# Batch 0's attention in a fused attention-and-convolution kernel: denominators, inverses and bias moved to other places in the order

## The chip, the cores and the metric

The kernel runs on one core of one Trainium2 chip. The metric is the device time of one execution in microseconds (us). The engines of the core work side by side, each through its own queue in order: TensorE (PE, matmuls), VectorE (DVE), ScalarE (ACT), GpSimd (POOL), and SyncE (SP), which issues transfers. ScalarE's and GpSimd's queues issue transfers as well. Engines wait for each other by semaphores.

## The reference

Two layers on an input of 4 images, 1024 channels, 32 x 32 pixels, all in float32. Cut to what matters:

```
# layer 0: self-attention over the 1024 pixels of each image, 16 heads of 64
qkv = x @ w_qkv.T + b_qkv
q, k = rmsnorm(rope(q)) * q_norm_w, rmsnorm(rope(k)) * k_norm_w
scores = einsum("bqhd,bkhd->bhqk", q, k) * hd**-0.5
ctx = einsum("bhqk,bkhd->bqhd", softmax(scores), v)
x = rmsnorm(ctx @ w_proj.T) * norm_out_w + x
# layer 1: bottleneck of convolutions 1x1, 3x3, 1x1
y = relu(bn(conv1x1(x, w1))); y = relu(bn(conv3x3(y, w2)))
x = relu(x + softplus(residual_scale) * bn(conv1x1(y, w3)))
```

The change touches the softmax and what follows it. The kernel computes exp(scores) without a shift, sums the exponentials over the keys (the denominator), multiplies the context by the inverse of the denominator, and adds the bias of v last, since the weights of a softmax sum to one.

## The kernel before

**Stages.** For each batch b of four, the kernel projects to q, k and v, runs the attention, and projects the context (y). Projections are done with fewer multiplications, by sums of operand and weight blocks formed on VectorE beforehand. Layer 1 follows after the four batches.

**Attention.** `attention` is called for each half c of the 1024 queries (`half[c]`, 512 queries), and loops over eight pairs of heads `hp`. One pass over (c, hp) is called a unit here; a batch has 16, numbered 0 to 15. In a unit, for eight tiles t of 128 keys, TensorE writes scores `sc` (L781), ScalarE exponentiates them to `p` (L788), and VectorE adds the tiles up to `den` (L799, L801). Then TensorE forms the contexts `cx` from v and p (L810). Two halves of the keys give two partial contexts: ScalarE copies the first to q's place (L816), and the second is copied and added by a GpSimd transfer (L819, L820), or, in the last unit, added by VectorE out of the context bank (L845).

**Denominators.** After every odd unit the sums of two units are a group. `sums_of_four` multiplies them with ones on TensorE (`dn`, L863). For most groups `inverses` does this: the step is put into `late`, and is run at tile t = 1 of the next unit. ScalarE copies the result (`rec`, L910), SP sends four rows to memory and reads them back spread over the partitions (`to_few`), VectorE inverts the few numbers (L914), and SP writes them back and broadcasts them to `inv` (`spread`, L932). The inversion waits in `half_done` until the end of a unit. `ready` then holds the broadcast rows, and at the end of the next odd unit `mean_of_v` multiplies the context by them on VectorE (L764) and adds v's bias on GpSimd (L765). The last group of the batch (`last_inverses`) inverts in place on VectorE (L924), and its means are formed in the projection (`means`, on VectorE).

**The projection's order.** `project2` issues products of eight matmuls each, counts half a unit of pace for each (`product_done`), and runs steps when their pace has come (`after`). In the first products: `start(0)` (bank p1, first ring of banks o1), `second(0)` (p2, ring o2), then the loop's first product into p1 and p5 (o2).

**Buffers.** PSUM has eight banks. In the attention three score tiles of two banks and a context tile of two use them all (`psum_for("att")`). The projections use two rings of four (`o1`, `o2`) in the same banks. The sums of a unit have two buffers in the pool `acc` ("tot"), and the exponentials have one buffer for each tile t, so that the next unit overwrites them.

**Other work in the stretch.** Batch 0's attention also prepares weights for later projections: `load_parts` (t = 3) loads four pieces over SP, and at a unit's end `extra` forms four sums on VectorE (L392 to L395), which GpSimd sends to memory (L397).

**What sets the order.** TensorE, GpSimd, VectorE and ScalarE run in the order in which the program is written there. SP's order is set by a scheduler when the program is built.

Of the kernel before, what the change touches and what calls it, by code (L numbers as in the profile page):

```python
# [11 lines left out]
F32 = mybir.dt.float32  # L12
AF = mybir.ActivationFunctionType
ALU = mybir.AluOpType
# [4 lines left out]
P = 128  # L19
# [4 lines left out]
NHP = C // (2 * HD)  # L24
CH = 512
NCH = N // CH
# [35 lines left out]
NH = NT // 2  # L62
# [23 lines left out]
def program(ctx, tc, x, wblk, w2, w3, vecs, cos, sin, out, bad):  # L86


    nc = tc.nc
# [26 lines left out]
    def col(name, i=0):  # L116
        return vec[:, COL[name] + i : COL[name] + i + 1]
# [40 lines left out]
    with tc.tile_pool(name=f"st{u}", bufs=2) as st, ExitStack() as s:  # L158

        tp = s.enter_context(tc.tile_pool(name=f"tp{u}", bufs=1))  # L160
# [24 lines left out]
        half = [slice(c * CH, (c + 1) * CH) for c in range(NCH)]  # L185
# [17 lines left out]
        def bank(kind, name):  # L203
            pool, shape = psum[kind]
            return pool.tile(shape, F32, tag=kind, name=name)
# [48 lines left out]
        def after(n, step):  # L254
            later.append((pace["at"] + n, step))
# [505 lines left out]
        def mean_of_v(q_all, c, hp, w, engine=nc.gpsimd):  # L761

            cx = q_all[:, hp, half[c]]
            nc.vector.tensor_tensor(cx, cx, w, ALU.mult)  # L764
            engine.tensor_scalar(cx, cx, col("bv", hp), None, ALU.add)  # L765

        def attention(b, c, q_all, k_all, v, probs_, late, ready, extra, slow, steps_in_all, load_parts, fold, then):


            at = half[c]  # L770
            sums_, contexts = [], []
            for hp in range(NHP):
                n = f"{b}_{c}_{hp}"
                rows = shifts(q_all, k_all, n, hp, c) if bad is None else None
                probs = []
                for t in range(N // P):
                    p = probs_[:, t]
                    sc = bank("sc", f"sc_{n}_{t}")
                    for keys in (low, high):
                        for j, d in enumerate((low, high)):  # L780
                            nc.tensor.matmul(  # L781
                                sc[keys, j], k_all[d, hp, t * P + keys.start : t * P + keys.stop], q_all[d, hp, at],
                                start=True, stop=bad is not None,
                            )
                    if bad is None:
                        for j in range(2):
                            nc.tensor.matmul(sc[:, j], ones[0:1, :], rows[j], start=False, stop=True)
                    nc.scalar.activation(p, sc, AF.Exp)  # L788
                    if t == 1:
                        if late:  # L790
                            late.pop(0)()
                        if fold and hp % 2 == 0:
                            d_ = fold[hp // 4][:, hp % 4 // 2 * 2 : hp % 4 // 2 * 2 + 2, :]
                        else:
                            d_ = acc.tile([P, 2, CH], F32, tag="tot", name=f"den_{n}")
                    if t == 3:
                        load_parts()
                    if t == 1:
                        nc.vector.tensor_tensor(d_, probs[0], p, ALU.add)  # L799
                    elif t > 1:  # L800
                        nc.vector.tensor_tensor(d_, d_, p, ALU.add)  # L801
                    probs.append(p)
                if (c, hp) == (NCH - 1, NHP - 1):
                    then()
                o = bank("cx", f"cx_{n}")
                for t in range(N // P):
                    for j in range(2):
                        h0 = (2 * hp + j) * HD
                        for i, keys in enumerate((low, high)):
                            nc.tensor.matmul(  # L810
                                o[j * HD : (j + 1) * HD, i], v[keys, t, h0 : h0 + HD], probs[t][keys, j],
                                start=(t == 0), stop=(t == N // P - 1),
                            )

                cx = q_all[:, hp, at]
                nc.scalar.copy(cx, o[:, 0])  # L816
                if b == 0 and (c, hp) != (NCH - 1, NHP - 1):
                    other = temp(f"cx_{n}")
                    nc.scalar.copy(other, o[:, 1])  # L819
                    nc.gpsimd.dma_start(cx, other, accum_op=ALU.add)  # L820
                else:
                    contexts.append((cx, o[:, 1]))
                sums_.append(d_)
                if hp % 2 == 1:
                    for r in ready:
                        mean_of_v(q_all, *r)
                    ready.clear()
                if fold:
                    halve(hp, d_, fold[hp // 4][:, hp % 4 // 2 * 2 : hp % 4 // 2 * 2 + 2, :])
                    if hp % 4 == 3:  # L830
                        eights.append((hp + 2, lambda n=n, hp=hp: sum_of_eight(b, n, hp, fold[hp // 4], ready)))
                if half_done and half_done[0][0] <= c * NHP + hp:
                    half_done.pop(0)[1]()
                if slow:
                    slow.pop(0)()

                if waiting:
                    next_waiting()
                slots = NCH * NHP - 1
                if extra and steps_in_all == 0 and hp > 0:  # L840
                    extra.pop(0)()
                for _ in range(len(extra) - -(-steps_in_all * max(slots - 1 - c * NHP - hp, 0) // slots) if steps_in_all else 0):
                    extra.pop(0)()
                if contexts:
                    nc.vector.tensor_tensor(contexts[0][0], *contexts.pop(0), ALU.add)  # L845
                if eights and eights[0][0] <= c * NHP + hp:
                    eights.pop(0)[1]()
                if hp % 2 == 0 or fold:
                    continue
                if (c, hp) == (NCH - 1, NHP - 1):  # L850
                    last_inverses(b, c, hp, n, sums_of_four(n, sums_), ready)
                else:
                    late.append(lambda n=n, hp=hp, ds=sums_: inverses(b, c, hp, n, sums_of_four(n, ds), ready))
                sums_ = []

        def sums_of_four(n, sums_):
            if n == f"0_{NCH - 1}_{NHP - 1}":
                bank("sc", f"skip_{n}")
            dn = bank("sc", f"dn_{n}")[:, 0]
            for i, d_ in enumerate(sums_):  # L860
                for j in range(2):
                    q = slice((2 * i + j) * QH, (2 * i + j + 1) * QH)
                    nc.tensor.matmul(dn[q, :], ones[:, :QH], d_[:, j], start=True, stop=True)  # L863
            return dn

        half_done, eights = [], []
        low, high = slice(0, P // 2), slice(P // 2, P)

        def halve(hp, d_, home):
# [35 lines left out]
        def inverses(b, c, hp, n, dn, ready):  # L905


            r = temp(f"rec_{n}")
            k = 2 * ((b * NCH + c) * NHP + hp - 1)
            nc.scalar.copy(r, dn)  # L910
            few, rows = to_few(n, k, 4, r[::QH, :])

            def invert():
                nc.vector.reciprocal(few, few)  # L914
                nc.sync.dma_start(rows, few)
                spread(c, hp, n, ready, [dens[k + j : k + j + 3 : 2, :] for j in range(2)])

            half_done.append((0, invert))

        def last_inverses(b, c, hp, n, dn, ready):  # L920
            k = 2 * ((b * NCH + c) * NHP + hp - 1)
            r = temp(f"rec_{n}")
            nc.scalar.copy(r, dn)
            nc.vector.reciprocal(r, r)  # L924
            nc.gpsimd.dma_start(dens[k : k + 4, :], r[::QH, :])
            spread(c, hp, n, ready, [dens[k + j : k + j + 3 : 2, :] for j in range(2)], nc.gpsimd)
# [271 lines left out]
        for b in range(B):  # L1198
# [29 lines left out]
            v = room  # L1228
# [30 lines left out]
            slow = [lambda: None] * 3 + [lambda f=f: add_residual(f) for f in range(NT)] if b > 0 else []  # L1259
            probs_ = xp.tile([P, N // P, 2, CH], F32, tag="x", name=f"p_{b}")  # L1260
            fold = [None, None]
            if b > 0:

                fold[0] = [tp.tile([P, NH, CH], F32, tag=t, name=f"den_{b}_{t}") for t in ("T0", "T2")]
# [8 lines left out]
            for c in range(NCH):  # L1273
                if (b, c) == (B - 1, NCH - 1):
                    extra = filters()
                attention(
                    b, c, q_all, k_all, v, probs_, late, ready, extra, slow, steps_in_all, load_parts, fold[c], then
                )
            psum_for("proj")
            room = v_room(f"to_{b}")  # L1280
# [50 lines left out]
        w = conv1_weights("last")  # L1331
# [364 lines left out]
```

## Time and profile before

| | us |
|---|---|
| median of three runs | 2651.2 |
| lowest and highest | 2650.92, 2652.52 |
| the profiled execution | 2650.94 |
| its span, first to last instruction | 2649.1 |
| batch 0's first score matmul (in the span) | 285.44 |
| batch 0's last context matmul group, start | 507.08 |
| first matmul of batch 0's output projection | 517.37 |

Times in the timelines count from the span's start. A line of a timeline gives the start, the duration from the first to the last end of the merged instructions, the engine, the line of the program, the operation with output and inputs, and in brackets the idle time before it and what ended that. Matmuls overlap: the next one starts before the one ahead has ended, so that the distance from start to start says more than a duration. In the page, a group's line ends with its idle time and the engine that ended most of it.

The table of waits of VectorE between 285 and 520 us (who waited for what: total us, times, longest):

```profile
DVE few L914 <- DMA few<-densf: 2.2, 2, 1.7
DVE w_pre L392 <- DMA w_pre<-in_wblk_dram: 2.2, 2, 1.2
```

VectorE waited four times in the whole stretch, for transfers alone.

### The profile page before, as it was taken

The numbers are of one execution on the slowest core, as the hardware profiler recorded it, in microseconds if no ns is written. First come the engines' busy times: TensorE is split into PE (matmuls) and PEld (weight loads), VectorE is DVE, ScalarE is ACT, GpSimd is POOL, SyncE is SP. The second block draws the span as 40 slices with busy tenths as digits, with TensorE's granted clock in tenths as the row PEclk, the third lists the DMA queues.
The fourth block names the chain that finished last, engine by engine and source line by source line (L and its number), as shares of the span: only waits on it lengthen the run. The fifth ranks groups of instructions, "written<-read, shape, count | busy, mean of one in ns | idle before, by whom it ended". The sixth has DMA issues, their size and how long they took to land. (4 is left out here: it accounts for less than half of the span.)

```text
span 2649.1 us, 40551 instructions
## 1 busy us (share of the span) xinstructions
PE 2626.4 (99%) x15446; PEld 1627.8 (61%) x15446; DVE 2143.2 (81%) x2595; ACT 1120.7 (42%) x1568; POOL 472.1 (18%) x592
## 2 busy tenths in 40 slices
PE   9999999999999999999999999999999999999997
PEld 4448533488888333688886333888884335846843
DVE  5567899998887877888879767987988779877987
ACT  2222566423442565333343565233525564312266
POOL 2542244301011221100111222000111221020000
PEclk9999999999999999999999999999999999999999
DMA  8887787777667451457775541765774443683175
GB/s 286 289 255 204 218 257 239 245 221 238 185 181 212 87 102 41 143 173 225 190 200 143 93 86 26 223 206 174 193 214 86 82 104 90 208 279 92 64 240 205
DMA packets 252939, 463.66 MB, mean 175 GB/s; under 512 B 32193, under 2 KB 125169, under 8 KB 252737
## 3 DMA queue, kind: packets, MB, share of 16 engines
q1 hardware_dynamic: 196816, 287.80, 34.7%
q0 software_dynamic: 47856, 156.40, 23.7%
q10 hardware_dynamic: 8064, 16.78, 1.8%
q8 instruction: 125, 2.05, 0.3%
q14 instruction: 78, 0.63, 0.1%
HBM read 329.53 MB, written 97.01 MB: 161 GB/s over the span
## 5 line engine op out<-in xcount | busy, mean ns | idle before, releaser
L788 ACT ACTIVATE p<-sc 128x1024 f32<-128x1024 f32 x512 | 478.2, 1047 | 17.7 <-PE sc L781 17.5
L781 PE MATMUL sc<-q,k 64*64 64x512 f32 x4096 | 456.4, 591 | 0.0
L801 DVE TENSOR_TENSOR den<-den,p 128x1024 f32<-128x1024 f32 x312 | 385.5, 1236 | 37.6 <-ACT p L788 5.1
L810 PE MATMUL cx<-p,to 64*64 64x512 f32 x3072 | 338.2, 589 | 0.0
L781 PEld LDWEIGHTS sc<-q,k 64*64 64x64 f32 x4096 | 149.3, 132 | 294.2 <-ACT p L788 150.6
L810 PEld LDWEIGHTS cx<-p,to 64*64 64x64 f32 x3072 | 117.5, 133 | 212.1 <-issue 210.8
L480 PE MATMUL p_v<-w_v,x 128*128 128x256 f32 x928 | 210.2, 379 | 1.4 <-DVE x L451 0.7
L485 PE MATMUL p_y<-q,w_y 128*128 128x256 f32 x928 | 209.8, 379 | 0.7 <-issue 0.7
L485 PEld LDWEIGHTS p_y<-q,w_y 128*128 128x128 f32 x928 | 176.0, 190 | 27.9 <-issue 4.1
L480 PEld LDWEIGHTS p_v<-w_v,x 128*128 128x128 f32 x928 | 176.1, 190 | 26.8 <-DVE x L451 1.7
L816 ACT COPY q<-cx 128x512 f32<-128x512 f32 x64 | 37.5, 586 | 348.0 <-PE cx L810 348.0
L765 POOL TENSOR_SCALAR q<-q,vec 128x512 f32<-128x512 f32 x56 | 110.1, 1985 | 290.2 <-DVE q L764 290.2
L485 PE MATMUL p_q<-to,w_q 128*128 128x256 f32 x672 | 152.2, 379 | 0.0
L485 PE MATMUL p_k<-to,w_k 128*128 128x256 f32 x672 | 152.2, 379 | 0.0
L485 PEld LDWEIGHTS p_q<-to,w_q 128*128 128x128 f32 x672 | 127.4, 190 | 18.4 <-issue 1.2
L485 PEld LDWEIGHTS p_k<-to,w_k 128*128 128x128 f32 x672 | 127.4, 190 | 18.4 <-issue 1.2
L810 PE MATMUL cx<-p,rq 64*64 64x512 f32 x1024 | 112.7, 589 | 0.0
L1600 PE MATMUL c<-h,w 128*128 128x512 f32 x256 | 110.3, 592 | 0.5 <-ACT h L1503 0.5
L799 DVE TENSOR_TENSOR den<-p 128x1024 f32<-128x1024 f32 x52 | 63.5, 1222 | 42.6 <-ACT p L788 42.6
L801 DVE TENSOR_TENSOR den_T<-den_T,p 128x1024 f32<-128x1024 f32 x72 | 88.2, 1225 | 7.5
L485 PE MATMUL p_y<-to,w_y 128*128 128x256 f32 x384 | 90.1, 379 | 0.6 <-PE p_y L485 0.6
L727 POOL DMA_DIRECT2D k<-ks x64 | 57.9, 1093 | 181.6 <-ACT p L788 70.9
(499 smaller groups left out, 4340.0 us busy)
## 6 DMA issues: line engine op xcount, KB each, us to landing
w_v<-wd2f SPq DMA_DIRECT2D x112, 256.0 KB, 3.2
w_y<-wd2f SPq DMA_DIRECT2D x112, 256.0 KB, 3.3
w_q<-wd2f SPq DMA_DIRECT2D x84, 256.0 KB, 3.0
w_k<-wd2f SPq DMA_DIRECT2D x84, 256.0 KB, 2.9
wd2f<-w_pre POOLq DMA_DIRECT2D x68, 256.0 KB, 4.5
q<-qs POOLq DMA_DIRECT2D x64, 256.0 KB, 5.5
k<-ks POOLq DMA_DIRECT2D x64, 256.0 KB, 4.7
x1df<-y POOLq DMA_DIRECT2D x32, 512.0 KB, 5.2
```

The costliest lines, as they stand in the source:

```text
L480: nc.tensor.matmul(o[:, q].rearrange("p (g f) -> p g f", g=2), r[:, i, q * P : (q + 1) * P], wt[:, :, i, :], skip_group_check=True, **at,)
L485: nc.tensor.matmul(o[:, q], wt[:, q, i, :], r[:, i, :], skip_group_check=True, **at)
L727: nc.gpsimd.dma_start(dst[i::2, f, :], other[1 - i :: 2, :], accum_op=ALU.add)
L765: engine.tensor_scalar(cx, cx, col("bv", hp), None, ALU.add)
L781: nc.tensor.matmul(sc[keys, j], k_all[d, hp, t * P + keys.start : t * P + keys.stop], q_all[d, hp, at], start=True, stop=bad is not None,)
L788: nc.scalar.activation(p, sc, AF.Exp)
L799: nc.vector.tensor_tensor(d_, probs[0], p, ALU.add)
L801: nc.vector.tensor_tensor(d_, d_, p, ALU.add)
L810: nc.tensor.matmul(o[j * HD : (j + 1) * HD, i], v[keys, t, h0 : h0 + HD], probs[t][keys, j], start=(t == 0), stop=(t == N // P - 1),)
L816: nc.scalar.copy(cx, o[:, 0])
L1600: nc.tensor.matmul(os[i], w3t[k][f // NH][:, f % NH, :], h2[b, k][:, half[c]], start=(k == 0), stop=(k == NPT - 1),)
```

## The change

All of it is in batch 0's attention and in the start of its projection; the other batches keep their order.

- The groups' denominators are formed after score tile t = 3 of the next unit in place of t = 1, but for the group whose next unit is 14.
- The sums of batch 0 get four buffers of their own, `own`, in the room of T0 and T2 (which hold operand sums of the projections before and after).
- The inversion of the few numbers comes at tile t = 2 of the odd unit after next, in place of the end of the unit before that; for the group of unit 13 it stays at the end of unit 14.
- The context is multiplied by the inverses at the end of even units in place of odd ones. The bias of v is added by ScalarE, behind the exponentials of tiles 5 and 6 of the next unit (`biases`). The group that is used in the last unit gets both steps from VectorE there.
- The last group's sums, inverses and broadcast (`last`) are put half a unit of pace into the projection, that is after its first product. Its sums go to a bank of the ring o2 in place of one of the score banks.

```diff
-        def attention(..., fold, then):
+        def attention(..., fold, then, own):
 ...
                     nc.scalar.activation(p, sc, AF.Exp)
+                    if t == (3 if b == 0 and (c, hp) != (NCH - 1, NHP - 2) else 1) and late:
+                        late.pop(0)()
+                    if t in (5, 6) and biases:
+                        biases.pop(0)()
+                    if b == 0 and t == 2 and half_done and half_done[0][0] < c * NHP + hp:
+                        half_done.pop(0)[1]()
                     if t == 1:
-                        if late:
-                            late.pop(0)()
-                        if fold and hp % 2 == 0:
+                        if b == 0:
+                            d_ = own[hp % 4 // 2][:, hp % 2 * 2 : hp % 2 * 2 + 2, :]
+                        elif fold and hp % 2 == 0:
 ...
-                if hp % 2 == 1:
+                if hp % 2 == min(b, 1) or (c, hp) == (NCH - 1, NHP - 1):
                     for r in ready:
-                        mean_of_v(q_all, *r)
+                        if b > 0:
+                            mean_of_v(q_all, *r)
+                        elif (c, hp) == (NCH - 1, NHP - 1):
+                            mean_of_v(q_all, *r, nc.vector)
+                        else:
+                            mean_and_bias(q_all, *r)
                     ready.clear()
 ...
                 if (c, hp) == (NCH - 1, NHP - 1):
-                    last_inverses(b, c, hp, n, sums_of_four(n, sums_), ready)
+
+                    def last(ds=sums_):
+                        last_inverses(b, c, hp, n, sums_of_four(n, ds), ready)
+
+                    if b == 0:
+                        after(0.5, last)
+                    else:
+                        last()
 ...
         def sums_of_four(n, sums_):
             if n == f"0_{NCH - 1}_{NHP - 1}":
-                bank("sc", f"skip_{n}")
-            dn = bank("sc", f"dn_{n}")[:, 0]
+                dn = bank("o2", f"dn_{n}")
+            else:
+                dn = bank("sc", f"dn_{n}")[:, 0]
 ...
-        half_done, eights = [], []
+        half_done, eights, biases = [], [], []
+
+        def mean_and_bias(q_all, c, hp, w):
+            cx = q_all[:, hp, half[c]]
+            nc.vector.tensor_tensor(cx, cx, w, ALU.mult)
+            biases.append(lambda: nc.scalar.activation(cx, cx, AF.Identity, bias=col("bv", hp)))
+
 ...
-            half_done.append((0, invert))
+            half_done.append((c * NHP + hp + (1.5 if hp < NHP - 3 or c < NCH - 1 else 1) if b == 0 else 0, invert))
 ...
+            own = None
+            if b == 0:
+                own = [tp.tile([P, NH, CH], F32, tag=t, name=f"den_{b}_{t}") for t in ("T0", "T2")]
```

More of the change, by code (lines that the diff above doesn't have):

```diff
@@ L765, in mean_of_v, with attention @@
             engine.tensor_scalar(cx, cx, col("bv", hp), None, ALU.add)
-        def attention(b, c, q_all, k_all, v, probs_, late, ready, extra, slow, steps_in_all, load_parts, fold, then):
+        def attention(b, c, q_all, k_all, v, probs_, late, ready, extra, slow, steps_in_all, load_parts, fold, then, own):
             at = half[c]
@@ L1276, in program @@
                 attention(
-                    b, c, q_all, k_all, v, probs_, late, ready, extra, slow, steps_in_all, load_parts, fold[c], then
+                    b, c, q_all, k_all, v, probs_, late, ready, extra, slow, steps_in_all, load_parts, fold[c], then, own
                 )
```

## The prediction

> **What bounds the kernel now.** I read the page first (busy shares, chain), then TensorE's waits, then the timelines of the five engines over batch 0's attention and the start of its projection, because the diff changes nothing else. The page:
>
> ```profile
> span 2649.1 us, 40551 instructions
> PE 2626.4 (99%) x15446; PEld 1627.8 (61%) x15446; DVE 2143.2 (81%) x2595; ACT 1120.7 (42%) x1568; POOL 472.1 (18%) x592
> ```
>
> TensorE is idle for 2649.1 - 2626.4 = 22.7 us in all, so a change that removes no TensorE work can gain only out of such gaps. Where they lie in the changed stretch, TensorE's timeline says (start, duration, instruction, idle before and its releaser):
>
> ```profile
> 343.54 1.07 PE L863 MATMUL dn<-den,ones 128*32 128x512 f32 x8
> 372.17 1.50 PE L863 MATMUL dn<-den,ones 128*32 128x512 f32 x8
> 373.60 5.38 PE L781 MATMUL sc<-q,k 64*64 64x512 f32 x48
> ...
> 507.08 7.05 PE L810 MATMUL cx<-p,rq 64*64 64x512 f32 x64
> 514.06 1.05 PE L863 MATMUL dn<-den,ones 128*32 128x512 f32 x4
> 515.58 1.05 PE L863 MATMUL dn<-den,ones 128*32 128x512 f32 x4 [0.47 <-DVE den L801]
> 517.37 3.69 PE L485 MATMUL p_y<-q,w_y 128*128 128x256 f32 x16 [0.73 <-issue]
> ```
>
> I number the 16 passes over (c, hp) as units 0 to 15. A denominator group normally takes 1.06 us with its pipelined tail and 1.0 us from start to start; only the one at 372.17 holds a wait of 0.43 us. The last group ought to end at 514.06 + 1.0 = 515.06 and the projection start then; it starts at 517.37. So 2.31 us are lost at the seam: 1.02 waiting for unit 15's denominators on VectorE, 1.29 until ScalarE's copy of the sums. Together 2.74 us is **all** there is to win here. The seam on VectorE and ScalarE:
>
> ```profile
> 507.65 7.87 DVE L801 TENSOR_TENSOR den<-den,p 128x1024 f32<-128x1024 f32 x6
> 515.44 0.69 DVE L450 TENSOR_TENSOR y<-q 128x512 f32<-128x512 f32 x1
> ...
> 518.05 1.29 DVE L764 TENSOR_TENSOR q<-q,inv 128x512 f32<-128x512 f32 x2
> 519.25 0.68 DVE L845 TENSOR_TENSOR q<-q,cx 128x512 f32<-128x512 f32 x1
> 519.85 3.35 DVE L924 RECIPROCAL rec<-rec 128x512 f32<-128x512 f32 x1
> ```
>
> ```profile
> 516.68 0.59 ACT L923 COPY rec<-dn 128x512 f32<-128x512 f32 x1 [1.90 <-PE dn L863]
> ```
>
> VectorE runs without a gap from 417.5 to 531; L845, which empties the last context bank, ends at 519.93. That number decides below.
>
> **What the Trainium skill says.** "SBUF — State Buffer", section "SBUF: two separate sides": VectorE and GpSimd share a port pair, an exclusive lock for the whole instruction when the VectorE operation has two SBUF inputs and the GpSimd one reads SBUF. The trace agrees: a 128x512 weight addition takes 0.69 us, but beside GpSimd's L765 it takes 1.05 to 1.18:
>
> ```profile
> 487.91 1.18 DVE L392 TENSOR_TENSOR w_pre<-w_pre,w_pre 128x512 f32<-128x512 f32 x1
> 489.12 0.69 DVE L393 TENSOR_TENSOR w_pre<-w_pre,w_pre 128x512 f32<-128x512 f32 x1
> 489.85 1.06 DVE L394 TENSOR_TENSOR w_pre<-w_pre,w_pre 128x512 f32<-128x512 f32 x1
> ```
>
> "ScalarE: Activation LUTs", section "Table sets: the hidden batching unit": cheap functions such as identity are in every set, so a bias between exponentials loads no table. No Identity stands between exponentials in this trace; the changed program's order shows no load added there. "Perfetto Trace Analysis", section "Identifying the Most-Contended Engine": matmul busy time is a poor measure, as matmuls are pipelined. The trace agrees: the seam's two idle marks say 1.20 us where start-to-start times say 2.31.
>
> **The change, part by part.** *Denominators at score tile 3 instead of 1* (six groups; the seventh, in unit 14, stays at tile 1). TensorE does the same matmuls. At 372.17 unit 5's sums were ready at 364.69 + 7.87 = 372.56; two tiles later the group starts at about 373.9, so 0.43 us goes and nothing takes its place. The other five cost and gain nothing. Cover: the group takes one of three score banks and its copy (0.6 us) stands behind two more exponentials. Exponentials follow each other by 7.46/8 = 0.93 us, score tiles by 6.87/8 = 0.86; the first starts 486.52 - 485.31 = 1.2 us after its unit. Counting from there, the exponential of tile 3 ends near 5.0, the copy near 5.5, and tile 6, which takes the copied bank, wants it at 6.15. If that 0.6 us of cover went, at most 0.2 to 0.3 us per group would show, 6 times.
>
> *Own buffers for the sums* (T0, T2) cost nothing: four instead of two, free since the value projection, and read out by 517, while the next batch writes them at 550.
>
> *Few inverses and their use later.* Per group the same small reciprocal (0.25 us), pair of multiplications (1.2 us) and five SP transfers (rows out, few in, few out, two broadcasts). The reciprocal now stands after tile 1's addition of the next odd unit, so VectorE's two waits for few (2.2 us) go. On SP the few transfers move past weight loads. The nearest case: the part that VectorE wants at 487.91 is loaded from 478.68 on, 8 transfers in 6.80 us with about 3 us to landing (as the page has it for w_y), so its four are there by about 485. VectorE will be there near 484.6, and needn't be before 485.3. Cover about 1 us; if gone, VectorE idles 1 to 2 us. The broadcast rows are wanted 15 us after their reciprocal and take about 9.
>
> *Bias of v by ScalarE.* 14 GpSimd operations of 1.97 us become 12 ScalarE ones and 2 VectorE ones. The nearest ScalarE row with a vector operand is L611 sq_q<-q,vec, 0.72 us; from below, the copies of L816, 0.59. I take 0.65, as neighbours overlap a little. They stand behind exponentials 5 and 6 of odd units, 1.3 us per unit, where ScalarE then sits idle for 5.3 us before the next context. The last tile is exponentiated near 10.1 us after the unit's start and wanted by the contexts at 6.87 + 7 x 0.86 = 12.9. Cost: nothing. Gain: VectorE's collisions. After its last wait (417.5) they cost 1.05 + 1.06 + 1.05 + 1.06 + 1.18 + 1.06 - 6 x 0.69 = 2.3 us before unit 15's sums are done, so these end at 515.52 - 2.3 = 513.2. From the other side: unit 14's sums can't start before its second exponential, about 3.25 us after the unit's start; its start (485.31 - 0.43) + 3.25 + 9.1 (sums) + 1.4 (multiplications, few) + 5.5 (two weight parts) + 9.1 = 513.2 too. Bounds: 512.1 (unit 15's own second exponential) and 515.5 (no gain).
>
> *Last group in the projection.* TensorE leaves the contexts at 514.06 - 0.43 = 513.63. The projection's first product needs no ScalarE copy now, and runs 1.73 us to 515.36; then the denominators, whose inputs are ready, to 516.36. They take the first bank of the second ring, so the **second product** gets the bank after it, which lies over the last context bank: in the changed program it waits for L845. Before the change that bank went to p5 (L563 on), three products further on at 517.37 + 3 x 1.73 = 522.6, when L845 was long done. L845 is itself later in VectorE's queue: the two bias operations of group 13 now stand ahead of it. Four such operations take 534.38 - 532.13 = 2.25 us in the later means, where two multiplications took 1.20, so 1.05 more. From the end of the sums to the end of L845 it was 519.93 - 515.52 = 4.41, and becomes 5.46. L845 ends at 513.2 + 5.46 = 518.66, and the second product starts near 518.75. Before, it started at 517.37 + 1.73 = 519.10. Queued behind this wait is the whole projection. **Net: 0.35 us gained**; 2.4 us of new waiting eats most of the 2.74.
>
> After that nothing is late: VectorE's long reciprocal starts near 518.7 (before 519.85), so the chain to the last means (VectorE waited 1.1 us at 532.13) is about 1 us earlier, TensorE only 0.35.
>
> Sum: the profiled execution took 2650.94 us (span 2649.1 and 1.84 around it), 0.26 below the median of 2651.2. 2651.2 - 0.35 = 2650.85, say 2650.9.
>
> **Rivals.** *The gate stays, and VectorE is not earlier* (slower). If removing GpSimd's reads frees nothing, or a weight part or the few of unit 14 (issued behind four weight loads on SP) come late by as much, unit 15's sums end at 515.5, L845 at 520.98, and the second product starts 1.95 us later than before: 2653.1. It decides from the point where L845 ends after 519.0. For it: the gap-free VectorE and the 1.05 us added to its queue. Against it: the collisions are in the trace, and the unit-14 account has its own bound.
>
> *No gate* (faster): if the second product didn't wait for L845, it would start at 516.36, 2.74 us earlier: 2648.5. For it: every removed wait is real. Against it: the wait stands in the changed program, and VectorE can't end L845 before 512.1 + 5.46 = 517.6, which leaves 1.45 us at best (2649.7).
>
> *The biases hold up the exponentials*: if they hit at every odd unit from 5 to 15 with the 1.3 us uncovered, 6 x 1.3 = 7.8 us: 2658.6. Only 2.8 us of cover speaks against it, but that is twice the cost.
>
> **How the numbers follow.** Gate with an earlier VectorE 0.62 (2649.6 to 2652.0); gate with VectorE as before 0.21; no gate 0.11; exponentials held up, or another wait above 5 us, 0.06. The range 2649.3 to 2653.4 takes in the first two and leaves out most of the rest. A difference of 0.2% is 5.3 us, about what a measurement of this kernel can tell from no change. All 2.74 us together are 0.10%, so faster by more needs a gap that this profile doesn't show: 0.02. Slower by more needs L845 after 524.4 or uncovered biases: 0.05. Within: 0.93.
>
> **What would show it.** Right: every denominator group at 1.06 us; no GpSimd L765 in batch 0 and weight additions at 0.69; one TensorE wait of 2 to 3 us for VectorE's L845 (L856 in the new numbering) in front of the second product, near 518.7. Wrong: that product near 516.4 (no gate) or near 521 (no earlier VectorE); TensorE gaps in score tiles of odd units; VectorE waiting for weight parts.

## The result, and the profile after

The changed kernel takes 2656.64 us (median of 22 runs, 2653.0 to 2660.61), the kernel before 2652.68 us beside it (22 runs, 2650.88 to 2655.74). The ratio is 1.0015, with a 95% interval of 1.0010 to 1.0021: about 4 us slower. That lies inside the 0.2% which the prediction calls about what can be told from no change, but outside its range of 2649.3 to 2653.4. The profiled execution of the changed kernel took 2655.39 us, 1.8 of it around this span:

```profile
span 2653.6 us, 40533 instructions
PE 2629.0 (99%) x15446; PEld 1629.8 (61%) x15446; DVE 2140.1 (81%) x2597; ACT 1127.5 (42%) x1580; POOL 446.9 (17%) x578
```

The span is 4.5 us longer. TensorE's busy time has grown by 2.6 us although it does the same 15446 matmuls. So a part of the loss is not waiting: the matmuls themselves took longer. TensorE's table of waits over the whole span (who waited for what: total us, times, longest) has one new entry of weight, and it is the first:

```profile
PE p_y L485 <- DVE q L856: 4.3, 1, 4.3
PE c2x L1489 <- DVE V L1424: 1.5, 2, 1.0
...
PE p_y L485 <- DMA w_y<-in_wblk_dram: 0.4, 1, 0.4
```

TensorE's timeline at the seam between attention and projection:

```profile
506.17 7.05 PE L816 MATMUL cx<-p,rq 64*64 64x512 f32 x64
513.63 1.97 PE L485 MATMUL p_y<-q,w_y 128*128 128x256 f32 x8 [0.42 <-DMA w_y<-in_wblk_dram]
515.53 1.81 PE L882 MATMUL dn<-den_T,ones 128*32 128x512 f32 x8
521.65 3.78 PE L485 MATMUL p_y<-q,w_y 128*128 128x256 f32 x8 [4.32 <-DVE q L856]
525.23 4.90 PE L485 MATMUL p_y<-y,w_y 128*128 128x256 f32 x16
529.96 1.89 PE L485 MATMUL p_y<-q,w_y 128*128 128x256 f32 x8
```

The first product, the denominators and then the second product behind the gate L856 stand where the prediction put them. But the second product starts at 521.65 in place of 518.75. And it takes 525.23 - 521.65 = 3.58 us from start to start, where a product takes 1.73; the next two take 529.96 - 525.23 = 4.73 in place of 3.45. The table by stretches says why. Each line gives a stretch and its length, then each engine's busy time in it, and in the column PEclk the granted TensorE clock. The stretches are cut where the record of the clock can step, every 3.41 us in this trace (the last section shows it); such a stretch is called a window from here on:

```profile
core 0: us, PE busy (x) PEld busy (x) DVE busy (x) ACT busy (x) POOL busy (x), PEclk, DMA share, GB/s
517.57:520.98 3.41, 0.00 (x0) 0.00 (x0) 3.34 (x7) 0.40 (x1) 0.00 (x0) 1.00 0.47 162
520.98:524.40 3.42, 2.75 (x7) 2.21 (x8) 3.42 (x3) 0.00 (x0) 0.00 (x0) 0.50 0.02 5
524.40:527.81 3.41, 3.41 (x10) 2.69 (x9) 3.38 (x4) 0.00 (x0) 0.58 (x1) 0.50 0.34 79
527.81:531.22 3.41, 3.41 (x17) 3.02 (x16) 3.28 (x5) 1.17 (x2) 1.21 (x2) 1.00 0.52 142
```

Behind a window without TensorE work the clock is at half for two windows, 6.83 us. The kernel before, with its two short waits at the seam, keeps it:

```profile
513.00:517.37 4.37, 3.17 (x21) 0.48 (x13) 4.16 (x5) 1.17 (x2) 0.00 (x0) 1.00 0.99 347
517.37:522.60 5.23, 5.23 (x24) 4.63 (x25) 5.23 (x6) 0.59 (x1) 3.48 (x2) 1.00 0.46 133
```

VectorE, whose L856 is the gate, shows no collision any more, but waits for transfers:

```profile
485.91 0.69 DVE L392 TENSOR_TENSOR w_pre<-w_pre,w_pre 128x512 f32<-128x512 f32 x1 [1.86 <-DMA w_pre<-wdf]
...
501.36 0.25 DVE L939 RECIPROCAL few<-few 128x16 f32<-128x16 f32 x1 [2.26 <-DMA few<-densf]
...
508.36 7.87 DVE L807 TENSOR_TENSOR den_T<-den_T,p 128x1024 f32<-128x1024 f32 x6
...
520.92 0.68 DVE L856 TENSOR_TENSOR q<-q,cx 128x512 f32<-128x512 f32 x1
```

The sums of unit 15 end at 508.36 + 7.87 = 516.2, and L856 at 521.6. The wait of 2.26 us is followed up on SP's queue, first after the change, then before it:

```profile
485.92 7.74 SPq L383 DMA_DIRECT2D w_pre<-wdf  x4
493.76 0.54 SPq L923 DMA_DIRECT2D densf<-rec  x1
494.42 1.63 SPq L383 DMA_DIRECT2D w_pre<-wdf  x3
496.37 0.33 SPq L927 DMA_DIRECT2D few<-densf  x1
```

```profile
488.98 0.53 SPq L898 DMA_DIRECT2D densf<-rec  x1
493.62 2.00 SPq L383 DMA_DIRECT2D w_pre<-wdf  x3
495.71 0.48 SPq L902 DMA_DIRECT2D few<-densf  x1
```

ScalarE had the sums (rec) of the group of unit 13 ready at 488.0. But they were issued at 493.76 only, since they stood on SP behind a weight load that waited for its buffer. Before the change they went out at 488.98. Even so the few themselves were read back only 0.66 us later than before (496.37 against 495.71), as then too they had stood behind weight loads. The larger part of the wait is that VectorE now came for them earlier: at 499.10, where before it came at 500.66 and found them there.

**One reading aid for what follows.** In a few of the profiled executions the stretch ahead of the attention runs up to 2 us longer: the changed kernel's first score matmul stands at 284.97 in one execution and at 287.05 in another, before the change at 285.44. So places at the seam are given here as distances from the first score matmul of batch 0. The n-th matmul of one trace is set against the n-th of another, with the denominators left out, as they were moved. "Fifth product" is the one at 524.35 in the kernel before.

| us after the first score matmul | first product | second | fifth | second to fifth |
|---|---|---|---|---|
| before | 231.93 | 233.73 | 238.91 | 5.18 |
| after | 228.67 | 236.69 | 244.99 | 8.30 |
| after, profiled again | 228.33 | 235.96 | 243.62 | 7.66 |

The gate costs 2.2 to 3.0 us at the second product; from the second to the fifth another 2.5 to 3.1 are lost to the clock. This agrees with the record of the clock: TensorE worked 2.75 + 3.41 = 6.16 us at half clock in the first trace and 1.44 + 3.42 = 4.86 us in the second (shown below), and half of that is 3.1 and 2.4. In the changed kernel's first trace the fifth product, by absolute times, is 5.6 us late and the last matmul 4.5. Most of that 1.1 is no gain of the change: the output projection of batch 3 lost it in the profiled execution of before (the matched difference falls from 5.62 to 4.55 between 2221 and 2246 us there), and the other traces, of kernels with and without the change, lack most of that loss too.

### The profile page after: what moved, and what is told of

It is laid out like the page before. It is cut to its first block, busy times and chain, and to the rows that moved or that the text cites. A ratio compares the mean times of both kernels' runs of the same rounds, so it can differ in the third digit from the quotient of the medians.

```text
span 2653.6 us, 40533 instructions
## 1 busy us (share of the span) xinstructions
PE 2629.0 (99%) x15446; PEld 1629.8 (61%) x15446; DVE 2140.1 (81%) x2597; ACT 1127.5 (42%) x1580; POOL 446.9 (17%) x578
## 5 line engine op out<-in xcount | busy, mean ns | idle before, releaser
L807 DVE TENSOR_TENSOR den<-den,p 128x1024 f32<-128x1024 f32 x216 | 267.6, 1239 | 27.6 <-ACT p L788 5.6
L807 DVE TENSOR_TENSOR den_T<-den_T,p 128x1024 f32<-128x1024 f32 x168 | 205.8, 1225 | 17.2 <-DVE den_T L807 0.5
L765 POOL TENSOR_SCALAR q<-q,vec 128x512 f32<-128x512 f32 x42 | 83.6, 2000 | 278.6 <-DVE q L764 278.6
L480 PE MATMUL p_v<-w_v,t 128*128 128x256 f32 x384 | 90.1, 379 | 0.0
```

What stands on the lines that cost most here:

```text
L480: nc.tensor.matmul(o[:, q].rearrange("p (g f) -> p g f", g=2), r[:, i, q * P : (q + 1) * P], wt[:, :, i, :], skip_group_check=True, **at,)
```

## The experiments

Theory 1 is the reading above: the loss is the gate, and the half clock that follows the idle stretch it makes. The rivals: the dip of the clock has nothing to do with the idle; the loss lies in the steps moved inside the attention, or in VectorE's new waits. All times are medians beside runs of the kernel before on the same chip. "Low clock" counts the runs whose mean clock over the span is 0.997 or less; 6.83 us at half clock take 3.4 of 2650 us, 0.0013, off the mean, and 3.41 us take 0.0006. In all 14 traces the mark is right (0.9963 to 0.9975 in the five with such a dip inside the span, 0.9975 to 0.9981 in the nine without), but for a short dip only narrowly. Before the change 3 of 169 runs are low.

| | edit on | us against before | ratio, 95% | second to fifth | low clock |
|---|---|---|---|---|---|
| after | - | +3.96 | 1.0015 (1.0010 to 1.0021) | 8.30 | 20 of 22 |
| after again | - | +3.45 | 1.0014 (1.0007 to 1.0021) | 7.66 | 18 of 19 |
| 32 fillers | after | +2.92 | 1.0014 (1.0007 to 1.0020) | 5.28 | 2 of 21 |
| 14 fillers | after | +0.47 | 1.0003 (0.9994 to 1.0011) | 5.29 | 2 of 13 |
| gate off | after | +1.70 | 1.0006 (1.0000 to 1.0013) | 5.28 | 5 of 21 |
| last group back | after | -0.20 | 1.0001 (0.9992 to 1.0009) | 5.18 | 1 of 13 |
| only last group | before | +0.69 | 1.0002 (0.9994 to 1.0011) | 5.26 | 4 of 13 |
| context first | after | -0.25 | 0.9999 (0.9990 to 1.0007) | 5.28 | 2 of 13 |
| few by GpSimd | after | +5.08 | 1.0019 (1.0011 to 1.0027) | 5.28 | 12 of 13 |
| all of these | after | +2.99 | 1.0013 (1.0006 to 1.0019) | - | 6 of 21 |
| no gate, SP kept | after | +1.21 | 1.0007 (1.0000 to 1.0013) | - | 6 of 21 |
| few by GpSimd | before | +1.63 | 1.0012 (1.0005 to 1.0019) | 5.18 | 10 of 21 |
| seam mended | before | -1.15 | 0.9998 (0.9990 to 1.0006) | - | 1 of 13 |

(In the three rows with "-" the denominators stand between these products.)

### The changed kernel again

> The changed kernel itself, beside the others on one chip. All theories: +3.5 to +4.5 us against the kernel before, mean clock 0.997 or less in most runs.

+3.45 us, 18 of 19 runs low. Its trace repeats the gate to the hundredth (4.32 us), and the half clock with it:

```profile
517.63:521.04 3.41, 1.06 (x8) 0.14 (x4) 3.34 (x6) 0.95 (x2) 0.00 (x0) 1.00 0.81 262
521.04:524.45 3.41, 1.44 (x4) 1.17 (x4) 3.38 (x5) 0.00 (x0) 0.00 (x0) 0.50 0.02 5
524.45:527.87 3.42, 3.42 (x10) 2.67 (x9) 3.38 (x3) 0.00 (x0) 0.58 (x1) 0.50 0.02 7
```

The loss is no accident of one execution. Here TensorE had still worked 1.06 us in the window ahead of the dip.

### Keep TensorE busy during the wait

```diff
                 dn = bank("o2", f"dn_{n}")
+                for _ in range(32):
+                    nc.tensor.matmul(dn[:, :P], ones, ones, start=True, stop=True)
```

> The changed kernel with 32 small matmuls of ones (128x128) put ahead of the last group's denominators, in the bank that these overwrite; the outputs are the same. They keep TensorE busy for about 3.4 us of the 4.3 us in which it waited for VectorE's L856. Theory 1 (the loss is the later second product, +2.55 us, plus a halved clock that follows an idle of over about 4 us, 3.1 us): the second product still starts near 521.6, the longest idle before it falls below 2 us, the granted clock stays at 1.0 behind it, and the time falls by about 3 us against the change, to the kernel before +0.5 to +1.5 us. Theory 2 (the dip of the clock has nothing to do with the idle, or the loss comes from the moved steps inside the attention): no gain, +4 us as in the change. Theory 3 (only the gate counts, the clock is made good later): also +4 us, but with the clock at 1.0.

The 32 matmuls took 7.31 us, twice the intended (the trace shows each as two records), and outlasted the gate: the second product started at 238.31. No dip followed (5.28 from second to fifth), but the fillers themselves gave the saving back: +2.92. Inconclusive for the time; for the clock it speaks for theory 1. Hence the same with 14:

> As the first filling run, with 14 small matmuls in place of 32 (32 took 7.31 us and overran the gate by some 3 us; 14 should take 3.2 us, and end before L856). Theory 1 (late second product plus halved clock after the idle): second product at the same distance from the start of the attention as in the change (236.7 us after the first score matmul, against 233.7 in the kernel before), idle before it about 2 us, mean clock 0.998 in nearly all runs where the change has 0.997 or less in 20 of 22, time about 3 us under the change: +0.5 to +1.5 us against the kernel before. Theory 2 (the clock does not matter, the later product does all): +3 to +4 us.

```profile
513.86 1.97 PE L485 MATMUL p_y<-q,w_y 128*128 128x256 f32 x8
515.66 3.29 PE L878 MATMUL dn<-ones 128*128 128x128 f32 x28
518.88 1.06 PE L884 MATMUL dn<-den_T,ones 128*32 128x512 f32 x8
520.62 1.99 PE L485 MATMUL p_y<-q,w_y 128*128 128x256 f32 x8 [0.67 <-DVE q L856]
```

The gate is still there, and the second product still late: 235.15, 1.4 us behind the kernel before. (It came 0.8 and 1.5 us earlier than in the two traces of the changed kernel, as VectorE waited only 0.65 us for few in this execution.) But TensorE computed through the wait, and the next products go at full speed: 5.29 us from second to fifth in place of 8.30 and 7.66, and 2 of 13 runs low in place of 20 of 22. The time is back to +0.47. These matmuls do nothing for the result, and the time falls by about 3 us: **the idle brings the dip**. The intervals of the two ratios still touch (0.9994 to 1.0011 against 1.0007 to 1.0021), so the clock counts and the traces carry this more than the time does. What a dip costs shows also with the program unchanged: in the five kernels of the table with at least four low runs and at least nine others, the low runs' median is 1.5 to 4.6 us above that of the others (a longer wait ahead of the dip may have a share in that).

### Take the gate away, or open it earlier

Another ring for the last denominators, so that the second product no longer gets the bank of the last context:

```diff
-                dn = bank("o2", f"dn_{n}")
+                dn = bank("o1", f"dn_{n}")
```

> The changed kernel with the last group's denominators in a bank of the first ring (o1) in place of the second (o2), so that the second product no longer lies over the last context bank; that bank then goes to p5, two products further on. Theory 1: the second product starts near 517.4 (behind the denominators, which wait for VectorE's sums until 516.2), p5 near 521.7 behind a wait of about 0.8 us, the clock stays at 1.0, and the time is about 1 us under the kernel before (-0.3 to -1.7). Theory 2 (the loss lies in the attention's moved steps): +3 to +4 us, as in the change.

The gate is gone: second product at 232.35, fifth at 237.63, 1.3 us ahead of the kernel before. The miss is +1.70 in place of -1. One part of it is in the trace: with the gate off, the next limit is close behind. The first product waits for its weights:

```profile
516.67 1.97 PE L485 MATMUL p_y<-q,w_y 128*128 128x256 f32 x8 [1.20 <-DMA w_y<-in_wblk_dram]
```

And the lead of 1.3 us isn't kept: when batch 1's attention starts (861 us), the matched matmuls stand 0.2 us behind those of the kernel before, 0.8 us of it from a wait for VectorE's L506. The profiled execution, at 2651.78 us, was among the best of the 21; 5 of them were low in clock. What those met can't be seen, as their traces are not kept.

The context's addition ahead of the last unit's means, in the changed kernel:

```diff
                     contexts.append((cx, o[:, 1]))
+                    if b == 0:
+                        nc.vector.tensor_tensor(contexts[0][0], *contexts.pop(0), ALU.add)
```

> The changed kernel with VectorE's addition of the last context (L856) put ahead of the last unit's four mean and bias operations (2.25 us). Theory 1: L856 ends 2.25 us earlier, the second product starts 234.4 us after the first score matmul (236.7 in the change), TensorE's idle is about 2.1 us, no halved clock in most runs; time +0.5 us (-0.5 to +1.5) against the kernel before. Theory 2 (gate and clock are not the cause): no gain, +4 us.

```profile
515.94 3.65 PE L485 MATMUL p_y<-q,w_y 128*128 128x256 f32 x8 [2.25 <-DMA w_y<-in_wblk_dram]
519.52 1.06 PE L884 MATMUL dn<-den_T,ones 128*32 128x512 f32 x8
520.86 1.99 PE L485 MATMUL p_y<-q,w_y 128*128 128x256 f32 x8 [0.28 <-DVE q L830]
```

The loss is gone (-0.25), as theory 1 has it: one VectorE instruction was moved ahead of 2.25 us of other work, and all else kept. The gate (L830 here) holds TensorE for 0.28 us in place of 4.32. But this execution waited 2.25 us for the first weights instead, and its first product then took 3.58 us (519.52 - 515.94) in place of 1.73: a dip of one window, after a much shorter idle.

```profile
512.55:515.97 3.42, 1.17 (x13) 0.21 (x5) 3.21 (x3) 0.58 (x1) 0.00 (x0) 1.00 0.98 343
515.97:519.38 3.41, 3.41 (x8) 2.44 (x8) 3.27 (x5) 0.00 (x0) 0.00 (x0) 0.50 1.02 369
```

Its fifth product stands at 240.71, 1.8 us behind the kernel before. It is one of the 2 low runs of 13; how the seam went in the others isn't shown.

### One part of the change at a time

The last group back at the end of the attention, the rest of the change kept:

```diff
-                    if b == 0:
-                        after(0.5, last)
-                    else:
-                        last()
+                    last()
```

(with the score bank for its sums, as before)

> The changed kernel with only the last group's step put back to the end of the attention, as before. Theory 1: no gate on the second product; the projection starts later than before by what the sums of unit 15 are later (516.2 against 515.5), so +0.5 to +1 us against the kernel before, and no dip of the clock. Theory 2 (moved steps inside the attention, biases on ScalarE, VectorE's new waits for transfers): most of the loss stays, +3 to +4 us.

```profile
514.08 1.05 PE L878 MATMUL dn<-den_T,ones 128*32 128x512 f32 x4
516.02 1.05 PE L878 MATMUL dn<-den_T,ones 128*32 128x512 f32 x4 [0.89 <-DVE den_T L807]
517.75 3.72 PE L485 MATMUL p_y<-q,w_y 128*128 128x256 f32 x16 [0.68 <-ACT rec L944]
```

-0.20 us, interval around 1. Everything else that the change does (later denominators, few, biases on ScalarE) together neither costs nor gains a measurable amount. At the seam it is a swap: the later sums of unit 15 cost about what the 0.43 us of unit 6 had brought.

The last group alone moved, on the kernel before:

```diff
-                    last_inverses(b, c, hp, n, sums_of_four(n, sums_), ready)
+                    if b == 0:
+                        after(0.5, last)
+                    else:
+                        last()
...
-                bank("sc", f"skip_{n}")
-            dn = bank("sc", f"dn_{n}")[:, 0]
+                dn = bank("o2", f"dn_{n}")
+            else:
+                dn = bank("sc", f"dn_{n}")[:, 0]
```

> The kernel before with only the last group moved into the projection, behind its first product, with its bank from the second ring. The sums of unit 15 end as before at 515.5, so L845 ends near 519.9 to 520.0 and the second product starts there, +0.9 us, behind a TensorE idle of 3.3 to 3.5 us. Theory 1 with the clock's limit above that idle: +0.9 us, clock 1.0. Theory 1 with the limit below it: about +4 us and a clock near 0.5 behind the idle. Theory 2 (loss in the rest of the change): 0 us.

+0.69 us, 4 of 13 runs low. In the trace the second product starts at 236.33, as late as in the changed kernel, but the dip is missing. The idle was split, 1.76 us for the first product's weights, then 1.64 ahead of the second, and no window was left nearly without work:

```profile
514.48:517.90 3.42, 1.66 (x12) 0.86 (x5) 3.15 (x4) 0.59 (x1) 0.00 (x0) 1.00 0.99 308
517.90:521.31 3.41, 2.05 (x13) 0.74 (x12) 3.41 (x6) 1.18 (x2) 0.91 (x1) 1.00 0.85 291
```

So the gate comes with the last group alone. In the changed kernel's two traces the first product starts 3 us earlier, and the waiting lies in one piece behind it.

### The transfers of the group of unit 13 on another queue

```diff
-            few, rows = to_few(n, k, 4, r[::QH, :])
+            few, rows = to_few(n, k, 4, r[::QH, :], nc.gpsimd if n == f"0_{NCH - 1}_{NHP - 3}" else nc.sync)
```

(`to_few` issues both of its transfers on the queue given)

> The changed kernel with the two transfers of the group of unit 13 (rec to memory, few back) on GpSimd's queue in place of SP's, where rec stood behind a weight load that waited for its buffer. Theory 1a (VectorE's 2.26 us wait for few is what made the sums of unit 15 end at 516.2 in place of the predicted 513.2): that wait goes, the sums end about 2 us earlier (229.2 us after the first score matmul in place of 231.2), L856 too, TensorE's idle falls from 4.3 to about 2.3 us, no halved clock, the time falls by 2 + 3 us: between -1.5 and +0.5 us against the kernel before. Theory 1b (something else follows close behind on VectorE, a weight part for one): the sums end less than 0.7 us earlier, the idle stays at 3.6 us or more, time +2.5 to +4 us.

A clear miss: +5.08 us. VectorE's wait for few fell from 2.26 to 0.58 us, but L856 came only 0.6 us earlier. The few themselves were there only 0.6 us earlier, 215.8 us after the first score matmul in place of 216.4: on GpSimd's queue the rows stood behind its stores until 492.28, and the few could be read back only at 497.94. The rest of the shorter wait is that VectorE came later, held up by other transfers (2.52 us for the few of an earlier group). The gate took 2.98 us, this time without a dip. The dip came later, in the value projection of batch 1, after a wait of 1.94 us:

```profile
517.10:520.52 3.42, 1.68 (x12) 0.41 (x10) 3.38 (x6) 1.17 (x2) 0.00 (x0) 1.00 0.86 291
520.52:523.93 3.41, 2.17 (x10) 1.94 (x11) 3.37 (x4) 0.00 (x0) 0.00 (x0) 1.00 0.04 10
827.71:831.12 3.41, 1.48 (x7) 0.97 (x6) 3.38 (x5) 0.59 (x1) 0.00 (x0) 1.00 0.68 197
831.12:834.53 3.41, 3.41 (x10) 2.69 (x9) 3.37 (x5) 0.59 (x1) 0.00 (x0) 0.50 0.08 14
```

All edits together: this one, the bank from the first ring, the context first, and the last group behind the second product:

```diff
-                        after(0.5, last)
+                        after(1, last)
```

> The changed kernel with the gate taken off in every way: last denominators behind the second product and in the first ring (o1), the last context added ahead of the means, and the two transfers of the group of unit 13 on GpSimd's queue. Theory 1: VectorE's last weight additions end 2 us earlier, so the projection's first weights (which load into the buffers these free) land by about 514 and no longer hold the first product; product 5 starts about 2.5 us earlier against the first score matmul than in the kernel before (236.4 us in place of 238.9), time -2.5 us (-3.5 to -1.0). If the first weights land no earlier than in the run with the gate off (229.5 us after the first score matmul): -1 us at most. Theory 2 (a loss inside the attention): +1 us or more.

At the seam this does what was expected: fifth product at 236.39, 2.5 us ahead of the kernel before. The time is +2.99 all the same. By matched matmuls the lead of 1.6 us (absolute) at the fifth product has become a lag of 1.4 by 592 us, 2.9 by 860, and 5.9 by 1722 us. Two runs take this apart. The same without the transfers on GpSimd's queue:

> The changed kernel with the last group behind the second product, its bank from the first ring, and the last context added ahead of the means: no gate left at the seam. All transfers stay on their queues. Theory A (the run that did the same and also moved two transfers to GpSimd's queue lost its 2.5 us later, through those transfers): the fifth product starts 1 to 1.5 us earlier against the first score matmul than before the change (the first weights bound it, 229.5 us after), little is lost later, time -1 us (-2 to +0.5). Theory B (an earlier projection runs into its own transfers in the batches that follow, whatever the queue): the gain at the seam is lost by the next attention, time +1 to +3 us.

And these transfers alone, on the kernel before:

> The kernel before with only the two transfers of the group of unit 13 (rec to memory, few back) on GpSimd's queue. Theory A: +2 to +5 us, in TensorE waits of the value projection of batch 1 or of the output projection of batch 2, as in the two runs with this edit. Theory B: within 0.7 us of the kernel before.

Both theories hold in part. Alone the queue edit makes 1.63 us, clear of no change, and less than theory A's 2 to 5. Between the two seam versions it makes 2.99 - 1.21 = 1.8 us, though these two intervals overlap. In the trace of the run with it alone, TensorE waits 1.6 us for VectorE in the value projection of batch 1, where the kernel before waits 0.7. That trace has also lost 1.8 us at the fifth product, but 1.3 of them by 420 us, before the two transfers go out (496.9 us), and up to there every queue runs in the order of before: that part is chance, and a single trace doesn't tell the rest from it. Of the 21 runs 10 are low in clock, where the kernel before beside them has 2 of 63, and their median is 3.0 us above that of the other 11; so a part of the cost seems to come by the clock. But also without this edit the gain at the seam is lost (+1.21), in the projection itself, 25 us later:

```profile
537.36 1.89 PE L485 MATMUL p_y<-y,w_y 128*128 128x256 f32 x8
541.45 2.68 PE L485 MATMUL p_y<-to,w_y 128*128 128x256 f32 x8 [2.19 <-issue]
543.91 2.91 PE L485 MATMUL p_y<-q,w_y 128*128 128x256 f32 x8
```

The product at 541.45 ought to start at 539.1; the window from 539.14 to 542.55 has 1.22 us of TensorE work, and the next is at half clock. The profile names no releaser for this wait. Why the queue edit costs some 1.6 us stays open too.

### The seam mended on the kernel before

The last group as in the run that moved it alone, but behind the second product and with a bank of the first ring, and the context first; the rest of the change left out:

```diff
+                    if b == 0:
+                        nc.vector.tensor_tensor(contexts[0][0], *contexts.pop(0), ALU.add)
...
+                        after(1, last)
...
+                dn = bank("o1", f"dn_{n}")
```

> The kernel before with only the seam mended: last group behind the second product, bank from the first ring, last context added ahead of the means. No gate. The first product waits for its weights (231.7 us after the first score matmul in the run that only moved the last group), so the fifth product starts at 239.6, against 238.9 in the kernel before: between -0.5 and +1.5 us. If the weights land by 229.5 as in the changed kernel: -1.5 us.

```profile
514.35 3.69 PE L485 MATMUL p_y<-q,w_y 128*128 128x256 f32 x16 [0.33 <-DMA w_y<-in_wblk_dram]
517.97 1.06 PE L873 MATMUL dn<-den,ones 128*32 128x512 f32 x8
```

No gate; the weights came at 229.45 in this execution, and the fifth product stands at 237.63, 1.3 us earlier than before. Of the absolute lead of 1.8 us, 1.3 is given back by the start of the next attention (0.8 of it in a wait for VectorE's L506). The median is 1.15 us below the kernel before, the lowest of all versions tried, but the ratio, 0.9998 (0.9990 to 1.0006), doesn't tell it from no change.

## Why the prediction was wrong, and where it was right

*Denominators at score tile 3:* right. The seven groups inside the attention take 1.06 or 1.07 us, the wait of 0.43 is gone, and in the matched matmuls unit 6 gains 0.44 us that nothing takes back inside the attention. *Own buffers* and *biases on ScalarE:* right. The biases (0.78 us each, predicted 0.65) stand behind the exponentials with no table load between (the one load of the stretch stands at 285.05, ahead of it), no TensorE wait comes of them, and with all but the last group kept the time is that of before. On the exclusive lock that the prediction cites for the collisions, the trace before agrees only in part: the addition at 487.91 was slowed to 1.18 us, but ended at 489.09, while the GpSimd operation beside it ran from 487.55 to 489.42 (times on GpSimd are rough). It shows that two slow each other, not that one shuts the other out for a whole instruction.

*The gate:* right in place and kind. From the end of the sums to the end of L856 it is 521.6 - 516.2 = 5.4 us, predicted 5.46.

**The step that failed is the sum under "Last group in the projection", twice.** First, its term "these end at 513.2" for the sums of unit 15. The collisions did go, every weight addition takes 0.69 us; but the sums ended at 516.2 (as distances from the first score matmul: 231.3 us, predicted 227.8). The prediction allowed a cover of about 1 us for the weight part of unit 13, with "1 to 2 us" if that were gone. It was gone (a wait of 1.86 us, 1.98 in the second trace). And it gave the few of unit 13's group no wait at all; but they were not there when VectorE, rid of the collisions, came for them: 2.26 us more (1.27 in the second trace). Between 417 us and the seam VectorE waited 6.7 us, where it had waited 1.2. The rival with the slower sign named just these two, and put L856 at 520.98, 235.5 us after the first score matmul, where 236.6 was measured. It had 0.21; on that mechanism it should have been the likeliest, as the four loads ahead on SP were seen. The second product is 2.55 us late by absolute times, 3.0 by distances, where 0.35 us of gain was forecast.

Second, a term that is missing in every case of the prediction: it counted 2.4 us of new TensorE waiting as 2.4 us of time. The wait became 4.3 us, and the clock was halved behind it, 2.5 to 3.1 us more. In the run with 14 fillers this term is gone (5.29 us from second to fifth product). The slower rival, 1.9 us above the prediction's starting point of 2651.2, stays below the measured difference of 3.96 us by 2.1, about as much. (That starting point, a median of three runs, was itself 1.5 us under the 2652.68 of the 22 runs beside the changed kernel; but counted from it, too, the range ended at +2.2 us.) The Trainium skill states it ("TensorE: Matmul & The Clock Gate", section "Part 1: The HAM clock gate (the "warmup" mystery)", under "What's actually happening"): the clock goes to half after about one idle window of some 3.4 us, and the window runs free of what the program does. The first trace agrees: one window of 3.41 us without work, then 0.50 for 6.83 us. The second shows that the window needn't be idle throughout: 1.06 us of work in it, and the same dip; the last section has the border.

*"All there is to win":* the 2.74 us were not to be had by taking the seam's waits away. With the gate off, the first product waited 1.20 us for its weights (1.76 and 2.25 in two other traces), and the seam gained 1.3. In the two traces where it didn't wait, the seam did gain 2.5, and later waits took it all. The account of the kernel before showed only the wait that came last at the seam, not the next one behind it.

## What to carry to other kernels

When a change gathers TensorE's idle time into one piece, price the clock as well as the wait: here waits of 1.76 and 1.64 us, apart, left it alone in the trace (4 of 13 runs are low), and one of 4.3 us cost 2.5 to 3.1 us more than itself. Before moving a step across a pool's boundary, list the bank that every later allocation of the ring gets, and for each the last reader of what lay there before; then move that reader forward (one VectorE instruction, put ahead of 2.25 us of other work, was worth the whole loss). And look for the wait behind the one that you remove, here the weights of the next stage, on the queue that issues them.

## What the runs showed of the hardware that was not expected

- The clock's record has two values, 1.00 and 0.50, and steps on a grid: inside the span each of the five dips lasts 3.41 or 6.83 us, and in each trace all the steps lie whole multiples of 3.41 us apart.
- What decides is how long TensorE worked within one window of that grid. The 14 traces hold some 10,800 windows (work is counted with the matmuls' modelled ends). At full clock, every window with at most 1.38 us of work (18, most of them at the kernel's end) was followed by half clock, and none with 1.57 us or more was; of the two between, the one with 1.48 was and the one with 1.44, at a kernel's end, wasn't. So the length of an idle doesn't decide alone, its place on the grid does too: 1.94 us in one window (1.48 us of work left) brought a dip, 2.98 us across two (1.68 and 2.17 us left) brought none.
- The grid lies elsewhere against the program in each execution: the window ahead of the dip starts 232.6 us after the first score matmul in one trace of the changed kernel, 230.6 us in the other. As an estimate from these figures: amid full work, an idle under 1.8 us (3.41 - 1.57) can't bring a dip, one over 4.1 us (2 x (3.41 - 1.38)) always does, and between them its place on the grid decides. The gate of 4.3 us lies above (38 of 41 runs low).
- A window at half clock that TensorE filled was the last one at half in all five dips; one with 2.75 us of work (changed kernel) and one with 1.44 us (its second trace) were not.
- Two small transfers, moved from SP's queue to GpSimd's, cost about 1.6 us (1.0005 to 1.0019) with the instructions of all engines, and SP's other transfers, in the same order, and made low clock more frequent (10 of 21 runs, 2 of 63 without). The cause stays open.
